# A two-layer attention kernel: an earlier first pair, later second-layer weights, a split last pair, and checks summed on ScalarE

## The chip, the cores and the metric

The kernel runs on one core of a Trainium2 chip. The metric is device time in microseconds (us), from the first to the last instruction of a run, and a median of several runs is quoted. All runs in this document, of both kernels and of every experiment, were in the fast state, so no slow run had to be set aside. The span of a profile is about 2 us shorter than the time of the same run; spans are compared with spans and times with times.

Five engines matter: TensorE (PE, and PEld for its weight loads), VectorE (DVE), ScalarE (ACT), SyncE (SP, which issues most transfers here) and the DMA engines. A wait of one engine for another is a semaphore wait. The profile also records the clock that TensorE was *granted*, as a share of full speed: 1.00 is full clock, 0.50 is half clock. A *fall* is a change from full to half.

## The reference

Two layers of the same form, one after the other, on four images of 128 channels by 96 x 96 positions. Every position attends to the 48 x 48 pooled keys of its image:

```python
g     = maxpool2(conv1x1(x, g_w, g_b))          # 64 channels, 2304 keys
theta = conv1x1(x, theta_w, theta_b)            # 64 channels, 9216 queries
phi   = maxpool2(conv1x1(x, phi_w, phi_b))      # 64 channels, 2304 keys
f     = einsum('bqc,bck->bqk', theta, phi)
y     = einsum('bqk,bkc->bqc', softmax(f), g)
W_y   = conv1x1(y, W_w, W_b)
inv   = bn_gamma * rsqrt(bn_var + BN_EPS)
out   = W_y * inv + (bn_beta - bn_mean * inv) + x
```

## The kernel before

The work is cut into 8 blocks (4 images times 2 layers, in an order that lets the layers of different images alternate). A block is 9 *pairs*; a pair is 1024 queries, held as two halves of 512 on the two halves of the partitions. A pair runs through 18 key tiles of 128 keys, two per step, so 9 steps. A step issues the score matmuls of two key tiles, their exponentials on ScalarE, the running sum of exponentials on VectorE, and one step later the value matmuls. Scores go to a PSUM pool of two buffers, so scores k + 2 need exponential k to be done.

When a pair ends, the next pair's first steps carry its ending: sum over keys (`denominators`), reciprocals and product (`normalise`), and four steps later the output projection (`project`). In the same place the keys of the next block are made bit by bit: 24 *chunks* of pooled projections, then *spread* into the layouts that the matmuls want. I call this place the *border* between two pairs.

```python
        def denominators(self):
            ps = ps_misc.tile([P, QT], F32, tag="misc", name=f"den_ps_{self.name}")
            for h in range(2):
                nc.tensor.matmul(ps[ts(h, CI), :], lhsT=ones, rhs=self.sum[:, ts(h, QT)],
                                 start=True, stop=True)
            self.rc = work.tile([P, QT], F32, tag="rc", name=f"rc_{self.name}", bufs=1)
            nc.scalar.copy(self.rc, ps)

        def normalise(self):
            rc, n = self.rc, self.number
            self.y = y = self.halves[:, :QT]
            nc.vector.tensor_add(y, y, self.halves[:, QT:])
            for i in range(QT // P):
                nc.vector.reciprocal(rc[:, ts(i, P)], rc[:, ts(i, P)])
            nc.vector.tensor_mul(y, y, rc)
            nc.vector.tensor_reduce(rmax[:, n : n + 1], rc, AX.X, ALU.max)   # checks
            nc.vector.tensor_reduce(rmin[:, n : n + 1], rc, AX.X, ALU.min)
# ... (the main loop, t counts steps of all pairs)
            if j == J_PROJECT and q:          # J_PROJECT = 4
                pairs[q - 1].project()
            if t <= total:
                for k in range(j * KB, (j + 1) * KB):
                    pairs[q].values(k)
            if j == J_WINDOW:                 # J_WINDOW = 0
                others = list(steps.pop(q % NP, [])) if q < len(pairs) else []
                if q:
                    pairs[q - 1].denominators()
                for step in others[:1]:
                    step()
                if q + 1 < len(pairs):
                    pairs[q + 1].theta()
                for step in others[1:]:
                    step()
                if q:
                    pairs[q - 1].normalise()
```

The checks find out whether a fixed shift of the exponent was safe for every query. If they fail, a general kernel runs afterwards; with these inputs it never does.

The instructions of TensorE, VectorE and ScalarE are issued in the order in which the program states them in the loop (it asks for a manual schedule). What stands early in the program therefore stands early in its engine's queue.

Of the kernel before, what the change touches and what calls it, by code (L numbers as in the profile page):

```python
# [37 lines left out]
CHUNKS = 3  # L38
ORDER = ((0, 0), (1, 0), (0, 1), (2, 0), (1, 1), (3, 0), (2, 1), (3, 1))
# [5 lines left out]
def shifted_blocks(ctx: ExitStack, tc: tile.TileContext, x: bass.AP, layers, out: bass.AP, flag):  # L45
# [26 lines left out]

    ident = const.tile([P, P], F32, name="ident")
# [7 lines left out]
    rmax = const.tile([P, len(ORDER) * NP], F32, name="rmax")  # L81
    rmin = const.tile([P, len(ORDER) * NP], F32, name="rmin")

    def load_x(b):
        xt = xp.tile([C, HW], F32, tag="x", name=f"x_{b}")
        src = x[b].rearrange("c h w -> c (h w)")
        n = 6
        for i in range(n):
            nc.sync.dma_start(out=xt[:, ts(i, HW // n)], in_=src[:, ts(i, HW // n)])
        return xt  # L90
# [4 lines left out]
    def column(src, name):  # L95
        t = const.tile([src.shape[0], 1], F32, name=name)
        nc.scalar.dma_start(out=t, in_=as_column(src))
        return t
# [10 lines left out]
    def load_layer(l, p):  # L109
        w = {}  # L110
        nat = prep.tile([CI, C], F32, tag="thnat", name=f"theta_nat_{l}")
        nc.scalar.dma_start(out=nat, in_=p["theta_w"])
        w["theta"] = transposed(nat, CI, C, f"thetaT_{l}")
        bias = const.tile([2 * CI, 1], F32, name=f"theta_b_{l}")
        for i in range(2):
            nc.scalar.dma_start(out=bias[ts(i, CI), :], in_=as_column(p["theta_b"]))
        w["theta_b"] = bias

        nat = prep.tile([2 * CI, C], F32, tag="wnat", name=f"gphi_nat_{l}")
        for i, key in enumerate(("g", "phi")):  # L120
            nc.scalar.dma_start(out=nat[ts(i, CI), :], in_=p[f"{key}_w"])
        w["gphi"] = transposed(nat, 2 * CI, C, f"gphiT_{l}")
        g_b = const.tile([P, CI], F32, name=f"g_b_{l}")
        nc.scalar.dma_start(
            out=g_b, in_=p["g_b"].rearrange("(o c) -> o c", o=1).to_broadcast((P, CI))
        )
        w["g_b"] = g_b

        W_b = column(p["W_b"], f"W_b_{l}")
        gamma = column(p["bn_gamma"], f"gamma_{l}")  # L130
        beta = column(p["bn_beta"], f"beta_{l}")
        mean = column(p["bn_mean"], f"mean_{l}")
        var = column(p["bn_var"], f"var_{l}")
        std = const.tile([C, 1], F32, name=f"std_{l}")
        nc.scalar.activation(std, var, AF.Sqrt, bias=eps)
        inv = const.tile([C, 1], F32, name=f"inv_{l}")
        nc.vector.reciprocal(inv, std)
        nc.vector.tensor_mul(inv, inv, gamma)
        shift = const.tile([C, 1], F32, name=f"shift_{l}")
        nc.vector.tensor_sub(shift, W_b, mean)  # L140
        nc.vector.scalar_tensor_tensor(shift, shift, inv, beta, op0=ALU.mult, op1=ALU.add)
        w["shift"] = shift

        W_nat = prep.tile([C, CI], F32, tag="Wnat", name=f"W_nat_{l}")
        nc.scalar.dma_start(out=W_nat, in_=p["W_w"])
        W_bn = prep.tile([C, CI], F32, tag="Wbn", name=f"W_bn_{l}")
        nc.vector.tensor_scalar(W_bn, W_nat, inv, None, ALU.mult)
        w["W"] = transposed(W_bn, C, CI, f"WT_{l}", twice=True)
        return w

    class Block:
# [5 lines left out]
        def begin_keys(self):  # L157
            name = self.name
            self.gphi = kvp.tile([P, NK], F32, tag="gphi", name=f"gphi_{name}", bufs=1)
            self.phi = kvp.tile([P, NK], F32, tag="phi", name=f"phi_{name}")  # L160
            self.gT = kvp.tile([P, NKT, CI], F32, tag="gT", name=f"gT_{name}")
            self.centre = kvp.tile([P, 1], F32, tag="centre", name=f"centre_{name}")

        def pooled(self, r):

            ps = ps_misc.tile([P, QT], F32, tag="misc", name=f"gphi_ps_{self.name}_{r}")
            for h in range(2):
                nc.tensor.matmul(  # L168
                    ps[ts(h, CI), :CC], lhsT=self.w["gphi"][:, ts(h, CI)],
# [9 lines left out]
        def spread(self, i):  # L179
# [3 lines left out]
            gphi, phi, centre = self.gphi, self.phi, self.centre  # L183
            keys = ts(i, GT * KT)
            if i == 0:
                nc.vector.tensor_reduce(centre[CI:, :], gphi[CI:, keys], AX.X, ALU.add)  # L186
                nc.vector.tensor_scalar(
                    centre[CI:, :], centre[CI:, :], -1.0 / (GT * KT), None, ALU.mult
                )
# [3 lines left out]
            nc.scalar.copy(phi[:CI, keys], phi[CI:, keys])  # L193
            ps = ps_misc.tile([P, QT], F32, tag="misc", name=f"gT_ps_{self.name}_{i}")
            for j in range(GT):
                nc.tensor.transpose(
                    ps[:, ts(j, CI)], gphi[:CI, ts(i * GT + j, KT)], ident[:CI, :CI]
                )
            nc.vector.tensor_tensor(
                self.gT[:, ts(i, GT), :],  # L200
                ps[:, : GT * CI].rearrange("p (t c) -> p t c", c=CI),
                self.w["g_b"].rearrange("p (o c) -> p o c", o=1).to_broadcast((P, GT, CI)),
# [3 lines left out]
        def key_steps(self):  # L206

            steps = {}
            for r in range(HW // CC):
                steps.setdefault(r // CHUNKS, []).append(lambda r=r: self.pooled(r))  # L210
            for i in range(NKT // GT):
                last = ((i + 1) * GT * KT * 4 // CC - 1) // CHUNKS
                steps.setdefault(last + 1, []).append(lambda i=i: self.spread(i))
            return steps

    class Pair:


        def __init__(self, blk, p, number):
            self.blk, self.p, self.number = blk, p, number  # L220
            self.name = f"{blk.name}_{p}"
            self.es = {}

        def theta(self):
            ps = ps_misc.tile([P, QT], F32, tag="misc", name=f"theta_ps_{self.name}")
            for h in range(2):
                nc.tensor.matmul(  # L227
                    ps[ts(h, CI), :], lhsT=self.blk.w["theta"],
# [3 lines left out]
            nc.scalar.activation(self.th, ps, AF.Identity, bias=self.blk.w["theta_b"])  # L232

        def scores(self, k):
# [14 lines left out]
            elif k > 1:  # L249
                nc.vector.tensor_add(self.sum, self.sum, e)  # L250

        def values(self, k):
            if k == 0:
                self.av = ps_av.tile([P, PT], F32, tag="av", name=f"av_{self.name}")
            e = self.es.pop(k)
# [7 lines left out]
            if k == NKT - 1:  # L263
# [3 lines left out]
        def denominators(self):  # L267
            ps = ps_misc.tile([P, QT], F32, tag="misc", name=f"den_ps_{self.name}")
            for h in range(2):
                nc.tensor.matmul(  # L270
                    ps[ts(h, CI), :], lhsT=ones, rhs=self.sum[:, ts(h, QT)],
                    start=True, stop=True,
                )
            self.rc = work.tile([P, QT], F32, tag="rc", name=f"rc_{self.name}", bufs=1)
            nc.scalar.copy(self.rc, ps)  # L275

        def normalise(self):
            rc, n = self.rc, self.number
            self.y = y = self.halves[:, :QT]
            nc.vector.tensor_add(y, y, self.halves[:, QT:])  # L280
            for i in range(QT // P):
                nc.vector.reciprocal(rc[:, ts(i, P)], rc[:, ts(i, P)])  # L282
            nc.vector.tensor_mul(y, y, rc)  # L283
            nc.vector.tensor_reduce(rmax[:, n : n + 1], rc, AX.X, ALU.max)  # L284
            nc.vector.tensor_reduce(rmin[:, n : n + 1], rc, AX.X, ALU.min)  # L285

        def project(self):
# [4 lines left out]
            for c in range(2):  # L292
                for h in range(2):
                    nc.tensor.matmul(  # L294
                        pss[h][ts(c, CI), :], lhsT=self.blk.w["W"][ts(h, CI), ts(c, CI)],
                        rhs=self.y[ts(h, CI), :], start=True, stop=True,
                    )
            for h in range(2):
                dst = self.blk.xt[:, ts(2 * self.p + h, QT)]
                nc.vector.scalar_tensor_tensor(  # L300
                    dst, pss[h], self.blk.w["shift"], dst, op0=ALU.add, op1=ALU.add
# [5 lines left out]
    xs = {0: load_x(0)}  # L307
    ws = [load_layer(l, p) for l, p in enumerate(layers)]
# [6 lines left out]
    def begin(n):  # L315
# [5 lines left out]
        blocks[n].begin_keys()  # L321

    begin(0)
    steps = blocks[0].key_steps()
    for n in sorted(steps):
        for step in steps[n]:
            step()

    pairs = [Pair(blk, p, n * NP + p) for n, blk in enumerate(blocks) for p in range(NP)]
    pairs[0].theta()  # L330
    total = len(pairs) * NB
    engines = {mybir.EngineType.PE, mybir.EngineType.DVE, mybir.EngineType.Activation}
    with tc.manual_schedule(engines=engines):
        for t in range(total + NB):
            if t < total:
                q, j = divmod(t, NB)
                if q % NP == 0 and j == 0 and q // NP + 1 < len(blocks):
                    begin(q // NP + 1)
                    steps = blocks[q // NP + 1].key_steps()
                for k in range(j * KB, (j + 1) * KB):  # L340
                    pairs[q].scores(k)
            if t == 0:
                continue
# [3 lines left out]
            if t <= total:  # L347
                for k in range(j * KB, (j + 1) * KB):
                    pairs[q].values(k)
            if j == J_WINDOW:  # L350
                others = list(steps.pop(q % NP, [])) if q < len(pairs) else []
# [8 lines left out]
                if q:  # L360
                    pairs[q - 1].normalise()

    bad = const.tile([P, 2], F32, name="bad")
    nc.vector.tensor_reduce(bad[:, 0:1], rmax, AX.X, ALU.max)
    nc.vector.tensor_scalar(bad[:, 0:1], bad[:, 0:1], 1.0 / SUM_MIN, None, ALU.is_gt)
    nc.vector.tensor_reduce(bad[:, 1:2], rmin, AX.X, ALU.min)
    nc.vector.tensor_scalar(bad[:, 1:2], bad[:, 1:2], 1.0 / SUM_MAX, None, ALU.is_lt)
    ps = ps_misc.tile([P, QT], F32, tag="misc", name="bad_ps")
    nc.tensor.matmul(ps[:1, :2], lhsT=ones[:, :1], rhs=bad, start=True, stop=True)
# [307 lines left out]
```

## Time and profile before

| | before |
|---|---|
| time, median of 3 runs | 2666.67 us (2666.65 to 2666.72) |
| span of the profile | 2666.4 us |
| TensorE busy | 2607.6 us, 98% |
| mean granted TensorE clock | 0.998 |
| period of a pair in the loop, most borders | 36.35 us |
| first exponential starts | 57.02 us |

The prediction shows the page's busy shares, the chain and the borders. Two rows of the table of costliest groups complete it. The columns are line, engine, operation, output<-input, shapes and count; then busy time in us and mean ns of one; then the engine's idle time just before them and what ended it.

```profile
L238 PE MATMUL sc<-theta,phi 64*64 64x512 f32 x10368 | 1234.2, 591 | 6.4 <-ACT exp L244 5.1
L258 PE MATMUL av<-exp,gT 64*64 64x512 f32 x10368 | 1228.8, 589 | 0.0
```

Scores and values are 2463 us of TensorE's 2608, both with nearly the same mean duration, 591 and 589 ns, and TensorE sat idle before the scores for 6.4 us only, in the whole kernel. These two means are worth keeping in mind: a TensorE matmul on a lower clock shows here.

### The profile page before, as it was taken

To read this page: it belongs to the slowest core of one execution; us is meant where nothing else is said; L and a number is where in the kernel's file an instruction comes from. 1 tells how busy PE (TensorE), PEld (TensorE's weight loads), DVE (VectorE), ACT (ScalarE), POOL (GpSimd) and SP (SyncE) were. 2 spreads that over 40 slices of the span, in tenths; PEclk is the share of its full clock that TensorE was granted. 3 is DMA by queue.
4 is the path that set the end of the run, shared out by engine and by line. 5 is a ranking of instruction groups with operands and counts; after the bars stand their busy time and mean duration, and the time that the engine had idled before them with its cause. 6 is when DMAs were issued, how large, how long until landed. Compare 5 with 4: busy or idle time off the path is not lost.

```text
span 2666.4 us, 51928 instructions
## 1 busy us (share of the span) xinstructions
PE 2607.6 (98%) x22808; PEld 896.0 (34%) x22808; DVE 2131.1 (80%) x2203; ACT 1576.9 (59%) x1564; POOL 0.7 (0%) x6
## 2 busy tenths in 40 slices
PE   5999999999999999999999999999999999999998
PEld 1333333333333333333333333333333333333332
DVE  3788787888877888787888778888787887888887
ACT  2655665656656656555665666655665656666664
POOL 0000000000000000000000000000000000000000
PEclk9999999999999999999999999999999999999999
DMA  6000000000000000100000000000000000000000
GB/s 218 1 1 1 1 1 1 1 1 1 1 9 17 17 17 12 77 1 1 1 1 11 15 17 17 17 1 1 1 1 1 17 17 9 17 17 17 17 17 26
DMA packets 11690, 41.48 MB, mean 16 GB/s; under 512 B 3392, under 2 KB 3776, under 8 KB 11456
## 3 DMA queue, kind: packets, MB, share of 16 engines
q1 hardware_dynamic: 8640, 37.75, 3.6%
q8 instruction: 180, 2.95, 0.5%
q10 hardware_dynamic: 2816, 0.34, 0.1%
q14 instruction: 54, 0.44, 0.1%
HBM read 19.21 MB, written 18.87 MB: 14 GB/s over the span
## 4 chain that ended last, share of the span: by engine, by line
PE 95%; ACT 3%; DMA 1%; DVE 1%; issue 0%; ACTq 0%
PE sc L238 42%; PE av L258 41%; PE gphi_ps L168 4%; PE theta_ps L227 3%; PE den_ps L270 3%; PE W_ps L294 2%; ACT theta L232 1%; DMA W_nat<-in_L_conv_W_w_dram 0%; ACT exp L244 0%; DVE centre L186 0%; ACT phi L190 0%; DVE gphi L172 0%; ACT phi L193 0%; DMA theta_b<-in_L_conv_theta_b_dram 0%; DMA theta_nat<-in_L_conv_theta_w_dram 0%
## 5 line engine op out<-in xcount | busy, mean ns | idle before, releaser
L244 ACT ACTIVATE exp<-sc,nshift 128x1024 f32<-128x1024 f32 x1296 | 1375.0, 1112 | 805.5 <-PE sc L238 805.3
L250 DVE TENSOR_TENSOR sum<-sum,exp 128x1024 f32<-128x1024 f32 x1152 | 1410.0, 1224 | 233.1 <-ACT exp L244 142.1
L238 PE MATMUL sc<-theta,phi 64*64 64x512 f32 x10368 | 1234.2, 591 | 6.4 <-ACT exp L244 5.1
L258 PE MATMUL av<-exp,gT 64*64 64x512 f32 x10368 | 1228.8, 589 | 0.0
L258 PEld LDWEIGHTS av<-exp,gT 64*64 64x64 f32 x10368 | 396.3, 133 | 716.1 <-issue 695.0
L238 PEld LDWEIGHTS sc<-theta,phi 64*64 64x64 f32 x10368 | 387.8, 133 | 726.4 <-issue 698.2
L282 DVE RECIPROCAL rc<-rc 128x128 f32<-128x128 f32 x288 | 243.4, 907 | 0.0
L172 DVE TENSOR_REDUCE gphi<-gphi_ps 128x96 f32<-128x384 f32 x192 | 107.0, 558 | 124.2 <-PE gphi_ps L168 123.5
L248 DVE TENSOR_TENSOR sum<-exp,exp 128x1024 f32<-128x1024 f32 x72 | 88.2, 1225 | 137.7 <-ACT exp L244 137.7
L168 PE MATMUL gphi_ps<-x,gphiT 128*64 128x384 f32 x768 | 160.5, 502 | 8.9 <-DVE gphi L172 0.7
L300 DVE SCALAR_TENSOR_TENSOR x<-W_ps,shift,x 128x512 f32<-128x512 f32 x144 | 101.0, 743 | 0.5 <-PE W_ps L294 0.5
L275 ACT COPY rc<-den_ps 128x512 f32<-128x512 f32 x72 | 42.2, 587 | 98.3 <-PE den_ps L270 98.3
L265 ACT COPY halves<-av 128x1024 f32<-128x1024 f32 x72 | 72.9, 1012 | 34.4 <-PE av L258 34.4
L232 ACT ACTIVATE theta<-theta_ps,theta_b 128x512 f32<-128x512 f32 x72 | 49.5, 687 | 69.4 <-PE theta_ps L227 69.2
L168 PEld LDWEIGHTS gphi_ps<-x,gphiT 128*64 128x64 f32 x768 | 48.7, 137 | 124.1 <-ACT theta L232 45.2
L227 PE MATMUL theta_ps<-x,thetaT 128*64 128x512 f32 x288 | 77.2, 614 | 3.4 <-ACT rc L275 1.2
L294 PE MATMUL W_ps<-halves,WT 64*64 64x512 f32 x576 | 75.7, 596 | 5.0 <-DVE halves L283 5.0
L270 PE MATMUL den_ps<-sum,ones 128*64 128x512 f32 x288 | 77.7, 618 | 0.0
L283 DVE TENSOR_TENSOR halves<-halves,rc 128x512 f32<-128x512 f32 x72 | 49.8, 692 | 2.5
L280 DVE TENSOR_TENSOR halves<-halves 128x512 f32<-128x512 f32 x72 | 49.1, 682 | 1.6 <-ACT halves L265 1.6
L284 DVE TENSOR_REDUCE rmax<-rc 128x1 f32<-128x512 f32 x72 | 48.9, 678 | 0.0
L285 DVE TENSOR_REDUCE rmin<-rc 128x1 f32<-128x512 f32 x72 | 48.6, 676 | 0.0
(45 smaller groups left out, 153.8 us busy)
## 6 DMA issues: line engine op xcount, KB each, us to landing
x<-in_x_dram SPq DMA_DIRECT2D x24, 768.0 KB, 9.1
out_dram<-x SPq DMA_DIRECT2D x36, 512.0 KB, 2.6
theta_nat<-in_L_conv_theta_w_dram ACTq DMA_DIRECT2D x2, 32.0 KB, 5.2
theta_b<-in_L_conv_theta_b_dram ACTq DMA_DIRECT2D x4, 0.2 KB, 5.9
gphi_nat<-in_L_conv_g_w_dram ACTq DMA_DIRECT2D x2, 32.0 KB, 5.3
gphi_nat<-in_L_conv_phi_w_dram ACTq DMA_DIRECT2D x2, 32.0 KB, 4.9
g_b<-in_L_conv_g_b_dram ACTq DMA_DIRECT2D x2, 32.0 KB, 5.1
W_nat<-in_L_conv_W_w_dram ACTq DMA_DIRECT2D x2, 32.0 KB, 6.8
```

The source lines that it names most:

```text
L168: nc.tensor.matmul(ps[ts(h, CI), :CC], lhsT=self.w["gphi"][:, ts(h, CI)], rhs=self.xt[:, ts(r, CC)], start=True, stop=True,)
L172: nc.vector.tensor_reduce(self.gphi[:, ts(r, CC // 4)].rearrange("p (h w) -> p h w", w=W // 2), ps[:, :CC].rearrange("p (h a w b) -> p h w ...
L227: nc.tensor.matmul(ps[ts(h, CI), :], lhsT=self.blk.w["theta"], rhs=self.blk.xt[:, ts(2 * self.p + h, QT)], start=True, stop=True,)
L238: nc.tensor.matmul(ps[ts(c, CI), ts(h, QT)], lhsT=self.blk.phi[ts(h, CI), ts(2 * k + c, CI)], rhs=self.th[ts(h, CI), :], start=True, stop= ...
L244: nc.scalar.activation(e, ps, AF.Exp, bias=nshift)
L248: nc.vector.tensor_add(self.sum, self.es[0], e)
L250: nc.vector.tensor_add(self.sum, self.sum, e)
L258: nc.tensor.matmul(self.av[ts(h, CI), ts(r, QT)], lhsT=self.blk.gT[ts(r, CI), k, :], rhs=e[ts(r, CI), ts(h, QT)], start=(k == 0), stop=(k ...
L270: nc.tensor.matmul(ps[ts(h, CI), :], lhsT=ones, rhs=self.sum[:, ts(h, QT)], start=True, stop=True,)
L282: nc.vector.reciprocal(rc[:, ts(i, P)], rc[:, ts(i, P)])
L294: nc.tensor.matmul(pss[h][ts(c, CI), :], lhsT=self.blk.w["W"][ts(h, CI), ts(c, CI)], rhs=self.y[ts(h, CI), :], start=True, stop=True,)
L300: nc.vector.scalar_tensor_tensor(dst, pss[h], self.blk.w["shift"], dst, op0=ALU.add, op1=ALU.add)
```

## The change

Its intent: fill the start, the end and VectorE's load. The first pair begins when 8 of the 24 chunks of keys are there, and the other 16 are made inside it. The whole program now runs under the manual schedule, SyncE included, where before only the loop did. The second layer's weights are prepared in the main loop. The last pair sums its denominators before its last values and goes out in two column halves. And the two check reductions of each pair leave VectorE: ScalarE sums denominators and reciprocals as by-products (`accum_out`) of passes over the same tile, one that was a copy before and one that is new. The diff, cut to its core:

```diff
         def denominators(self):
...
             self.rc = work.tile([P, QT], F32, tag="rc", name=f"rc_{self.name}", bufs=1)
-            nc.scalar.copy(self.rc, ps)
+            if self.last:
+                self.inverses(ps)
+            n = self.number
+            nc.scalar.activation(
+                self.th if self.last else self.rc, ps, AF.Identity,
+                accum_out=dens[:, n : n + 1],
+            )
+        def note(self):
+            n = self.number
+            to = self.th if self.last else self.rc
+            nc.scalar.activation(to, self.rc, AF.Identity, accum_out=recs[:, n : n + 1])
 
         def normalise(self):
-            rc, n = self.rc, self.number
             self.y = y = self.halves[:, :QT]
             nc.vector.tensor_add(y, y, self.halves[:, QT:])
-            for i in range(QT // P):
-                nc.vector.reciprocal(rc[:, ts(i, P)], rc[:, ts(i, P)])
-            nc.vector.tensor_mul(y, y, rc)
-            nc.vector.tensor_reduce(rmax[:, n : n + 1], rc, AX.X, ALU.max)
-            nc.vector.tensor_reduce(rmin[:, n : n + 1], rc, AX.X, ALU.min)
+            self.inverses(self.rc)
+            nc.vector.tensor_mul(y, y, self.rc)
+            self.note()
...
-    begin(0)
-    steps = blocks[0].key_steps()
-    for n in sorted(steps):
-        for step in steps[n]:
-            step()
...
+    begin(0, FIRST_GT)
+    b0 = blocks[0]
+    ws[0].make_gphi()
+    b0.pooled(0)
+    b0.pooled(1)
+    b0.pooled_2(2)
+    b0.spread_phi(0)
+    ws[0].make_theta()
+    pairs[0].theta()
+    b0.pooled_2(4)
+    b0.pooled_2(6)
+    b0.spread_phi(1)
+    b0.spread_g(0)
+    between = {0: 8, 1: 12, 3: 16, 4: 20}
+    after = {
+        0: [lambda: b0.spread_g(1)],
...
+        NB: [ws[1].make_gphi, ws[1].make_theta],
+        2 * NB: [ws[1].make_shift],
+        2 * NB + 1: [ws[1].make_W],
+    }
...
+            if t == total - 1:
+                pairs[-1].denominators()
+            if t == total:
+                break
...
+    pairs[-1].finish(check, result)
```

## The prediction

> **What bounds the kernel now.** I read the page first: busy shares, then the chain of work that ended last.
>
> ```profile
> PE 2607.6 (98%) x22808; PEld 896.0 (34%) x22808; DVE 2131.1 (80%) x2203; ACT 1576.9 (59%) x1564; POOL 0.7 (0%) x6
> ...
> PE 95%; ACT 3%; DMA 1%; DVE 1%; issue 0%; ACTq 0%
> ```
>
> TensorE (PE) is busy for 2607.6 of 2666.4 us and is 95% of the chain. All other idle time together is 58.8 us, 2.2% of the span. So whatever shortens the start and the end can save 2.2% at the very most, and anything that makes TensorE wait inside the loop is paid in full. I therefore looked at three places: the start, the end, and one border between two pairs.
>
> The start, from the chain in order of time:
>
> ```profile
> 20.01 9.17 DMA W_nat<-in_L_conv_W_w_dram
> ...
> 29.52 0.42 PE WT_ps L102
> 29.93 5.80 PE gphi_ps L168 x20
> ...
> 55.73 1.28 ACT L244
> 57.02 1.12 ACT exp L244
> ```
>
> All weights of both layers are prepared before the first chunk of keys (29.9 us), all 24 chunks are made before the first score, and the first exponential runs at 57.02. The first five chunks take 5.80 us, against 1.51 us for two (0.76 each) later: TensorE starts at half speed.
>
> A border between two pairs, from the timeline (the whole argument rests on it):
>
> ```profile
> 1193.92 1.95 PE L238 MATMUL sc<-theta,phi 64*64 64x512 f32 x16
> ...
> 1195.08 2.12 ACT L244 ACTIVATE exp<-sc,nshift 128x1024 f32<-128x1024 f32 x2 [2.00 <-PE sc L238]
> 1195.11 3.38 DVE L282 RECIPROCAL rc<-rc 128x128 f32<-128x128 f32 x4
> ...
> 1195.69 1.90 PE L258 MATMUL av<-exp,gT 64*64 64x512 f32 x16
> ...
> 1197.40 1.90 PE L238 MATMUL sc<-theta,phi 64*64 64x512 f32 x16
> ...
> 1198.52 0.69 DVE L283 TENSOR_TENSOR halves<-halves,rc 128x512 f32<-128x512 f32 x1
> ...
> 1199.12 1.04 PE L258 MATMUL av<-exp,gT 64*64 64x512 f32 x8
> ```
>
> Columns are start, duration, engine, line. Scores 4 and 5 start at 1193.92, exponentials 4 and 5 at 1195.08, and scores 6 and 7 at 1197.40 because the exponentials have freed the two score buffers in PSUM (the pool has two). The normalisation of the pair before runs on VectorE meanwhile and ends at 1198.52 + 0.69 = 1199.21. Here nobody waits for it.
>
> The same kernel has one border per block where ScalarE is held up: it must first shift the keys by a centre that VectorE computes.
>
> ```profile
> 1156.53 1.95 PE L238 MATMUL sc<-theta,phi 64*64 64x512 f32 x16
> 1158.30 1.90 PE L258 MATMUL av<-exp,gT 64*64 64x512 f32 x16
> 1160.86 2.09 PE L238 MATMUL sc<-theta,phi 64*64 64x512 f32 x16 [0.67 <-ACT exp L244]
> 1162.77 1.90 PE L258 MATMUL av<-exp,gT 64*64 64x512 f32 x16
> ```
>
> In the same view exponential 4 starts there only at 1159.69. Scores 6 follow it by 1.17 us and the value matmuls by 3.08 us (1162.77 - 1159.69). Without the delay they would start 1199.12 - 1193.92 = 5.20 us after scores 4, at 1161.73; that border lost 1.04 us. So a late ScalarE does reach TensorE, and 1.17 and 3.08 are the measured rule.
>
> **What the Trainium skill says.** "TensorE: Matmul & The Clock Gate", section "Architectural detail: the array is 16× 32×32, not 1× 128×128", says that the queues of ScalarE and VectorE are strictly first in, first out. The border just shown agrees: exponentials whose scores were there stood behind the shift that waited. The same page, section "What's actually happening", puts TensorE at half clock after an idle window of about 3.4 us that runs freely. The trace agrees: idle from about 2651.8, the granted clock falls from 1.00 to 0.50 at about 2656.2, and the last eight projection records take 1.98 us there, against 1.04 in the loop. "ScalarE: Activation LUTs", section "What ACT_TABLE_LOAD costs", gives 186 ns + 0.833 ns per element, 93 ns more for a pointer operand, and 1283 ns per table load. The trace has 587 ns for a copy of 512 columns, 687 ns with a bias, and 1.28 us per load. What the accumulator output costs, neither says.
>
> **The change part by part.**
>
> *Checks on ScalarE.* VectorE loses two reductions per pair (678 + 676 ns). It was not the bound, so this gains nothing. ScalarE gains one pass over the reciprocals per pair. The compiled order of the changed kernel shows where:
>
> ```
> L313 Activation rc, dens <- den_ps
> L265 Activation theta <- theta_ps
> L325 Activation rc, recs <- rc       [waits DVE, Activation]
> L277 Activation exp 4 <- sc 4        [waits PE]
> ```
>
> The pass stands ahead of exponentials 4 and 5 and waits for VectorE. It also writes the reciprocals in place, and the product that ends the normalisation reads them, so it must wait for that product as well, to 1199.21. (In the compiled program of the first such border it waits for VectorE's count 73, the same count on which the projection, which reads the product, waits.) In the border above: handover 0.04 us (the gap between centre and shift in the trace), pass 0.65 us (an estimate from 587 and 687 ns), so exponential 4 starts at about 1199.90 instead of 1195.08. By the rule the value matmuls start at 1199.90 + 3.08 = 1202.98 instead of 1199.12: **3.86 us lost**. The borders with other extra work give nearly the same by the same steps: with the centre 1163.74 + 3.08 - 1162.77 = 4.05; with the second part of the keys (product at 1271.72, value matmuls at 1272.33) 3.85; without keys, in the last block (reciprocals from 2625.17, scores 4 at 2623.98), 3.86. Only where the third part is spread and no chunk is made (product at 1341.51, value matmuls at 1343.37) it is 2.60. There are 71 such borders, 7 of the last kind: 64 x 3.86 + 7 x 2.60 = **265 us**. Later work can't win it back: the rest of a pair runs at the pace of TensorE.
>
> *The clock.* TensorE would idle from 1197.59 to 1199.90 + 1.17 = 1201.07, 3.48 us. That is barely one window of 3.41 us (the page's 4096 cycles), so a complete idle window falls into few gaps; each would cost about 1.7 us (half of 3.41). If a tenth did, I get some **8 us** over 71 borders (2 to 60).
>
> *Denominators.* The copy out of PSUM becomes an activation with accumulator, about 0.15 us longer (687 - 587, plus something for the accumulator). The theta matmul takes that buffer next; its weight load already waits for the copy at 56 borders. About 60 x 0.15 = **9 us**.
>
> *The start.* Layer 1's weights leave it, the first pair needs 8 chunks, and ScalarE still issues a dozen transfers and loads two tables. With weights at about 4 us, four chunks at half speed (1.3 each), ScalarE free at about 14, then two shifts, theta: first exponential at about 17.6 instead of 57.02, 39 us earlier. Given back inside the first pair: 16 chunks of 0.65 us (10.4), transposes and weights (2.5), and waits of a loop with extra work on all engines (5, a guess). Net **-22 us**. The 24 chunks of the next block are only packed differently (4 in six borders).
>
> *The end.* Before, 15.6 us pass from the last value matmuls (2650.8) to the end, of which the reciprocals take 3.38. Now they run beside the last value matmuls, but two more denominator matmuls (0.86) precede those. Projection, addition and store in halves overlap a little. I take **-2 us**; the 6 us from the flag (2660.5) to the end stay.
>
> Sum: 2666.7 + 265 + 8 + 9 - 22 - 2 = about **2925 us**, 9.7% slower.
>
> **The rivals.**
> - *The wait is hidden and only start and end count*: 2666.7 - 24 = 2643, within 2%. For it speaks ScalarE's 59% load. Against it: its idle time lies in the wrong place, and the order of a strict queue decides, not the average.
> - *The pass waits for the reciprocals alone*, not for the product: exponentials start 0.6 us earlier, 71 x 0.6 = 43 us less, 2880. The in-place write and the count speak against it.
> - *Nearly every gap trips the clock*: 71 x 1.7 to 3.4 us more, 3035 to 3160. The gap sits at the limit, so this is the large risk upwards.
> - *VectorE was the hidden bound*, and its 1.36 us per pair come back: 98 us. Against it: in the loop the view of waits shows TensorE itself waiting for ScalarE (4.0 us) and never for VectorE; the weight loads that wait for VectorE's sums before the denominators run ahead of the matmuls.
>
> **Range and chances.** The pass (0.1 us either way, 7 us in all), the accumulator (8), start and end (6) and the clock (0 to 60) give 2890 to 2975. Slower by over 2% needs only a quarter of the stall; I give it 0.92. Within 2%, if the stall is hidden, 0.05. Faster by over 2% would need nearly all of TensorE's idle time, 0.03.
>
> **What would show it.** Right: at each border exponential 4 starts just after the new pass, the pass idles on the product of the normalisation for about 5 us, TensorE idles 3.5 us waiting for the exponential (some 230 us in all where it now shows 4.0), the pair takes about 40.2 us instead of 36.4, and the first exponential is at 15 to 20 us. Wrong: exponentials 4 and 5 still start 1.2 us after their scores, or the pass waits for nothing; then the time lies near 2643. A granted clock of 0.5 after the gaps would show the third rival.

## The result, and the profile after

| | before | after |
|---|---|---|
| time, median of 4 runs each | 2666.69 us (2666.65 to 2667.74) | 3041.53 us (3037.84 to 3042.95) |
| ratio of fast runs | | 1.1402 (95%: 1.1383 to 1.1422) |
| span of the profile | 2666.4 us | 3040.8 us |
| mean granted clock | 0.998 | 0.950 |
| first exponential | 57.02 us | 24.71 us |
| first scores to second pair's first scores | 55.76 to 89.33 us | 22.66 to 81.30 us |
| second to last pair | 2526.67 us | 2904.49 us |
| last pair's first scores to the end | 50.37 us | 54.97 us |

A ratio here is the mean time of one kernel's fast runs over that of the other's of the same rounds, so it is not quite the ratio of the quoted medians.

The kernel is 14.0% slower. The prediction said slower, with 2925 us, but the time lies 66.5 us above the upper end of its range, 2975. The table says where the time is: the second pair starts 8.0 us earlier, the loop from there to the last pair takes 377.8 us longer, and the last pair with the end 4.6 us longer (it holds one more border). The sum is 374.4.

The same rows of the page as before, with the busy line and the row of the new pass (L325):

```profile
PE 2760.7 (91%) x22822; PEld 894.1 (29%) x22822; DVE 2057.1 (68%) x2067; ACT 1636.2 (54%) x1786; POOL 0.7 (0%) x6
...
L271 PE MATMUL sc<-theta,phi 64*64 64x512 f32 x10368 | 1335.1, 634 | 235.0 <-ACT exp L277 235.0
L291 PE MATMUL av<-exp,gT 64*64 64x512 f32 x10368 | 1259.8, 603 | 0.0
...
L325 ACT ACTIVATE rc<-rc 128x512 f32<-128x512 f32 x71 | 44.7, 629 | 363.4 <-DVE halves L331 363.4
```

There are two things to see. The new pass costs only 44.7 us of ScalarE, but ScalarE stood idle for 363.4 us before it, waiting for VectorE's product (L331), and TensorE waited 235.0 us for exponentials where it was 5.1. That is the predicted wait, at nearly the predicted size (some 230). But TensorE is also *busier*: 2760.7 us against 2607.6, with practically the same number of instructions. The scores' mean rose from 591 to 634 ns and the values' from 589 to 603. No instruction became larger; the granted clock fell.

A border in the middle of the kernel, from the timeline (start and duration in us, engine, line, count of records; in brackets the idle time before and its releaser):

```profile
1352.54 1.95 PE L271 MATMUL sc<-theta,phi 64*64 64x512 f32 x16
...
1357.14 0.69 DVE L331 TENSOR_TENSOR halves<-halves,rc 128x512 f32<-128x512 f32 x1
1357.93 0.63 ACT L325 ACTIVATE rc<-rc 128x512 f32<-128x512 f32 x1 [6.24 <-DVE halves L331]
1358.46 0.19 ACT L325 ACTIVATION_READ_ACCUMULATOR rc<-rc 128x1 f32 x1
1358.56 2.10 ACT L277 ACTIVATE exp<-sc,nshift 128x1024 f32<-128x1024 f32 x2
1359.70 3.45 PE L271 MATMUL sc<-theta,phi 64*64 64x512 f32 x16 [3.50 <-ACT exp L277]
```

The scores of 1352.54 are ready by about 1354.5. Their exponentials start at 1358.56, right behind the pass, which starts 0.10 us after the product has ended (1357.14 + 0.69 = 1357.83). TensorE idles 3.50 us. Then the next sixteen score records take 3.45 us where the same sixteen took 1.95 us before the gap. Busy time and granted clock of TensorE in four stretches of 3.41 us, the period with which the clock's changes fall in this trace (columns: stretch, length, busy time and count, clock, DMA share, GB/s):

```profile
1352.54:1355.96 3.42, 3.42 (x34) 1.00 0.00 0
1355.96:1359.37 3.41, 0.24 (x4) 1.00 0.00 0
1359.37:1362.78 3.41, 3.08 (x16) 0.50 0.03 5
1362.78:1366.20 3.42, 3.42 (x36) 1.00 0.00 0
```

The gap does not fill a stretch: TensorE was busy for 0.24 us of the second one. Yet the third was granted half the clock. And this is no rarity at the edge; here is another border where the gap was only 2.08 us (TensorE stopped 1.33 us into the stretch that starts at 1902.09):

```profile
1902.09:1905.50 3.41, 1.33 (x18) 1.00 0.00 0
1905.50:1908.91 3.41, 3.41 (x16) 0.50 0.02 5
```

A stretch with 1.33 us of work in it, 39%, was followed by one at half clock. Over the whole trace there are 68 times at half clock, each but the last one or two stretches long, 304.8 us together. Before had 12.5 us, all at the end. (Each of these sums, and those below, runs some 2 us past the last instruction, and the record of the clock begins only at 24.75 us here and at 34.79 before.) Each of the 68 falls followed a stretch at full clock, and the busy share of that stretch was between 0.01 and 0.42. Not one was wholly idle.

At the start, VectorE's order inside the first pair shows another loss, which matters later:

```profile
26.86 1.23 DVE L281 TENSOR_TENSOR sum<-exp,exp 128x1024 f32<-128x1024 f32 x1 [3.65 <-ACT exp L277]
28.00 1.48 DVE L192 TENSOR_REDUCE gphi<-gphi_ps 128x96 f32<-128x384 f32 x3
29.53 0.87 PE L188 MATMUL gphi_ps<-x,gphiT 128*64 128x384 f32 x4 [1.83 <-DVE gphi L192]
```

VectorE waits 3.65 us for exponentials, sums them, and only then takes the maxima of chunks that were already in PSUM. TensorE waits behind it for a free buffer.

### The profile page after: what moved, and what is told of

The parts are those of the page before. It is cut to its first block, busy times and chain, and to the rows that moved or that the text cites. A ratio compares the mean times of both kernels' runs of the same rounds, so it can differ in the third digit from the quotient of the medians.

```text
span 3040.8 us, 51534 instructions
## 1 busy us (share of the span) xinstructions
PE 2760.7 (91%) x22822; PEld 894.1 (29%) x22822; DVE 2057.1 (68%) x2067; ACT 1636.2 (54%) x1786; POOL 0.7 (0%) x6
## 4 chain that ended last, share of the span: by engine, by line
## 5 line engine op out<-in xcount | busy, mean ns | idle before, releaser
L271 PE MATMUL sc<-theta,phi 64*64 64x512 f32 x10368 | 1335.1, 634 | 235.0 <-ACT exp L277 235.0
L291 PE MATMUL av<-exp,gT 64*64 64x512 f32 x10368 | 1259.8, 603 | 0.0
L325 ACT ACTIVATE rc<-rc 128x512 f32<-128x512 f32 x71 | 44.7, 629 | 363.4 <-DVE halves L331 363.4
L313 ACT ACTIVATE rc<-den_ps 128x512 f32<-128x512 f32 x71 | 42.4, 597 | 98.1 <-PE den_ps L305 98.1
L331 DVE TENSOR_TENSOR halves<-halves,rc 128x512 f32<-128x512 f32 x71 | 49.1, 692 | 2.4
L214 ACT ACTIVATE phi<-gphi,centre 64x768 f32<-64x768 f32 (+1 forms) x27 | 23.2, 859 | 28.4 <-DVE centre L213 21.0
```

Of the source, the lines that this page charges most:

```text
L271: nc.tensor.matmul(ps[ts(c, CI), ts(h, QT)], lhsT=self.blk.phi[ts(h, CI), ts(2 * k + c, CI)], rhs=self.th[ts(h, CI), :], start=True, stop= ...
L291: nc.tensor.matmul(self.av[ts(h, CI), ts(r, QT)], lhsT=self.blk.gT[ts(r, CI), k, :], rhs=e[ts(r, CI), ts(h, QT)], start=(k == 0), stop=(k ...
```

## The experiments

Eight kernels ran in two calls. The first four share one chip and the runs of the kernel before on it (median 2667.66 us, 2663.38 to 2671.46, 15 runs); the other four share another (2666.77 us, 2661.99 to 2669.2, 16 runs). All eight gave correct results. An earlier form of e3, with a tile of its own for the pass, did not build for want of on-chip memory and became the form below (that build is not on record).

My theory: the place of the new pass in ScalarE's queue costs everything, in two ways, a direct wait and a clock that falls in the gap it leaves. Rivals: that the other parts of the change (start, second layer's weights, end) cost something; that only a gap that fills a whole stretch of 3.41 us trips the clock; that the clock is a side show and the direct wait larger than I worked out; that relieving VectorE is worth something by itself.

### e1: the pass four steps later

```diff
@@ normalise
             nc.vector.tensor_mul(y, y, self.rc)
-            self.note()
@@ main loop
             if j == J_PROJECT and q:
+                pairs[q - 1].note()
                 pairs[q - 1].project()
```

> The changed kernel with ScalarE's pass over the reciprocals issued four steps later, when VectorE has long finished. My theory (the pass stands ahead of two exponentials in ScalarE's queue and waits for the normalisation; the gap that this makes in TensorE also drops its clock) expects the whole loss of the loop to go: 2655 to 2672 us, TensorE waiting under 10 us for exponentials in the loop, and half clock in the trace for under 30 us instead of 305. Rival, that the extra ScalarE work or the accumulator itself costs the time: still over 2900. Rival, that start and end lost it: the same, over 2900.

Measured: 2665.39 us (2663.11 to 2669.19, 12 runs), ratio to before 0.9994 (0.9985 to 1.0003). The clock is back at 0.997. A border of this kernel, from the timeline:

```profile
1332.04 2.11 ACT L277 ACTIVATE exp<-sc,nshift 128x1024 f32<-128x1024 f32 x2
...
1333.91 0.69 DVE L331 TENSOR_TENSOR halves<-halves,rc 128x512 f32<-128x512 f32 x1
1334.15 1.90 PE L271 MATMUL sc<-theta,phi 64*64 64x512 f32 x16
...
1344.13 0.63 ACT L325 ACTIVATE rc<-rc 128x512 f32<-128x512 f32 x1
```

The exponentials no longer wait for the product: they start 1.87 us before it. The pass runs ten microseconds after it, when its input has long been there, and nobody waits. One line moved in the program takes 376 us back (3041.53 - 2665.39). So the whole loss was the place of the pass, and the work of the checks on ScalarE is nearly free. In the loop the period of most pairs is 36.45 us, against 36.35 before; e5 shows that this 0.10 us is what the accumulator in `denominators` leaves on the path.

It also shows what the rest of the change is worth: 2.3 us by the medians, which the interval doesn't tell from nothing. In its trace the second pair starts 13.6 us earlier than before (75.71 against 89.33), the loop takes 8.9 us longer (2535.56 against 2526.67), and the last pair with the end 0.6 us less (49.75 against 50.37).

### e2: the checks alone, on the kernel before

```diff
@@ denominators
-            nc.scalar.copy(self.rc, ps)
+            n = self.number
+            nc.scalar.activation(self.rc, ps, AF.Identity, accum_out=dens[:, n : n + 1])
@@ normalise
-            nc.vector.tensor_reduce(rmax[:, n : n + 1], rc, AX.X, ALU.max)
-            nc.vector.tensor_reduce(rmin[:, n : n + 1], rc, AX.X, ALU.min)
+            nc.scalar.activation(rc, rc, AF.Identity, accum_out=recs[:, n : n + 1])
```

(and the judging of the sums at the end, as in the change.)

> The kernel before with the checks on ScalarE and nothing else. If the checks carry the whole loss and the other parts gave some 8 us back at the start: 3040 to 3058 us, with the same gaps of 3.4 to 3.5 us. If the new first pair or the new order of the other engines is needed for the loss: near 2667.

Measured: 3054.39 us (3050.06 to 3056.08), ratio 1.1455 (1.1436 to 1.1474). The granted clock is 0.95 here too, with some 315 us at half clock. Its view of waits (total us, times, longest):

```profile
ACT rc L285 <- DVE halves L284: 362.8, 71, 6.5
```

The same 71 waits with the same total as in the changed kernel (363.4). This part alone makes the loss. The other parts together don't add to it.

### e3: the pass waits for the reciprocals only

```diff
@@ note
-            to = self.th if self.last else self.rc
+            to = self.th if self.last else self.halves[:, QT:]
             nc.scalar.activation(to, self.rc, AF.Identity, accum_out=recs[:, n : n + 1])
```

The pass now writes where the product doesn't read, into the half of `halves` that has been added already, so it needn't wait for the product. It still stands at the same place in the queue.

> The changed kernel, but the pass writes into a tile that nobody reads, so it waits for the reciprocals and not for the product behind them (0.69 us). My theory: the gaps shrink by about 0.6 us to 2.9, 43 us less direct waiting, and the clock still falls at most borders because a window need only be 60% idle: 2970 to 3005 us. If the clock fell only in gaps longer than its window of 3.41 us, the clock's part would go as well: 2850 to 2870. If the product were not what it waits for: 3041.

Measured: 2953.2 us (2947.79 to 2958.06), ratio 1.1075 (1.1054 to 1.1096). That is 88 us less than the changed kernel, more than I expected.

```profile
PE sc L271 <- ACT exp L277: 183.7, 71, 3.9
```

TensorE's direct wait fell from 235.0 to 183.7 us over the same 71 borders, 0.72 us each, the product's duration and handover. Most gaps are 2.78 us long now. If only gaps beyond 3.41 us tripped the clock, only the few with a longer gap would, and the time would lie at 2850 to 2870; but half-clock time is still 219 us, in 55 times. My miss was the other way: the time lies 17 us below my range of 2970 to 3005. Gaps of 2.7 to 2.8 us tripped almost as often as the longer ones, 43 of 46. But in the last block, where gaps are 1.57 us, none did, and only 7 times in the loop did half clock last two stretches, against 19 in the changed kernel.

### e4: the gaps filled with idle-time matmuls

```diff
+    def busy(q, n):
+        ps = ps_misc.tile([P, QT], F32, tag="misc", name=f"busy_ps_{q}")
+        for _ in range(n):
+            nc.tensor.matmul(ps[:CI, :], lhsT=ones, rhs=pairs[q].th, start=True, stop=True)
@@ main loop, after the values of the step
+            if j == 1 and 0 < q < len(pairs):
+                busy(q, 1 if q % NP == NP - 1 or q >= total // NB - NP else 3)
```

The order, the pass and its wait are those of the changed kernel. Nothing reads the three (or one) added matmuls per border; they only keep TensorE busy where it would idle. This takes the clock away and leaves the wait.

> The changed kernel with three idle-time matmuls (one where the gap is 2.1 us) put into each gap of TensorE; they write a buffer that nobody reads and fit into the gap. The wait itself stays. If the half clock costs about 150 us of the loss: 2885 to 2920 us with half clock for under 60 us in all. If the clock is a by-product that costs nothing (the matmuls behind the gap would wait anyway): 3035 to 3060.

Measured: 2925.35 us (2923.78 to 2928.93), ratio 1.0967 (1.0948 to 1.0985), clock 0.995, 31 us at half clock. That is 5 us above the upper end of what I expected: the clock was worth less than the 150 us I had put on it.

```profile
1308.74 2.79 PE L451 MATMUL busy_ps<-theta,ones 128*64 128x512 f32 x6
1311.16 2.10 ACT L277 ACTIVATE exp<-sc,nshift 128x1024 f32<-128x1024 f32 x2
1312.31 2.09 PE L271 MATMUL sc<-theta,phi 64*64 64x512 f32 x16 [0.78 <-ACT exp L277]
```

The gap is filled for 2.79 us, 0.78 us remain, and the scores behind it take 2.09 us instead of 3.45. Useless work made the kernel 116 us faster (3041.53 - 2925.35). That is the price of the clock, a little low, as 7 of the 68 falls are still there. What remains, 260 us (2925.35 - 2665.39), is the price of the direct wait and of those falls. By the periods of the pairs, e4 less e1:

| border | predicted loss, us | measured, us |
|---|---|---|
| most (36.45 -> 40.33) | 3.86 | 3.88 |
| with the centre (38.00 -> 42.02) | 4.05 | 4.02 |
| second part of the keys (36.97 -> 40.78) | 3.85 | 3.81 |
| third part, no chunk (34.80 -> 37.26) | 2.60 | 2.46 |
| last block (33.79 -> 36.46) | 3.86 | 2.67 |

The second row is that of the four blocks whose clock stayed up; in the three others it fell there, and the loss was 5.6 to 5.7 us. The last row was off: I had taken the border of the very last pair, which has no theta matmul, for all of the last block's.

### e5: the checks back on VectorE

From the changed kernel, the checks of all pairs but the last are again a maximum and a minimum on VectorE; start and end stay as changed.

```diff
@@ denominators
+            else:
+                nc.scalar.copy(self.rc, ps)
@@ note
-            to = self.th if self.last else self.rc
-            nc.scalar.activation(to, self.rc, AF.Identity, accum_out=recs[:, n : n + 1])
+            if self.last:
+                nc.scalar.activation(self.th, self.rc, AF.Identity, accum_out=recs)
+                return
+            nc.vector.tensor_reduce(rmax[:, n : n + 1], self.rc, AX.X, ALU.max)
+            nc.vector.tensor_reduce(rmin[:, n : n + 1], self.rc, AX.X, ALU.min)
```

(The judging of these maxima and minima also moves, to three steps before the end.)

> The changed kernel with the checks of the first 71 pairs back on VectorE as before; start and end stay as changed. If VectorE's two reductions cost nothing and the accumulator's read costs 0.1 us at 56 borders: about 6 us below the kernel with the late pass, 2655 to 2663 us, 0.2 to 0.4% under the kernel before. If VectorE's relief is worth something: slower than the kernel with the late pass.

Measured: 2661.19 us (2655.27 to 2662.31, 13 runs), ratio 0.9976 (0.9967 to 0.9984). VectorE is at 80% here and at 77% in e1, and e5 is not slower but some 4 us faster. The two ran on different chips, so the medians alone would not carry the 4 us. The loops of the two profiles do: most pairs take 36.35 us here, as before, and 36.45 in e1, and from the second to the last pair e5 takes 2529.32 us, 6.2 less than e1. The place of the 0.10 us, first in e1 and then here:

```profile
1144.61 0.60 ACT L313 ACTIVATE rc<-den_ps 128x512 f32<-128x512 f32 x1 [1.39 <-PE den_ps L305]
1145.10 0.19 ACT L313 ACTIVATION_READ_ACCUMULATOR rc<-den_ps 128x1 f32 x1
...
1145.35 1.08 PE L260 MATMUL theta_ps<-x,thetaT 128*64 128x512 f32 x4
```

```profile
1147.14 0.59 ACT L316 COPY rc<-den_ps 128x512 f32<-128x512 f32 x1 [1.39 <-PE den_ps L307]
...
1147.77 1.08 PE L262 MATMUL theta_ps<-x,thetaT 128*64 128x512 f32 x4
```

The theta matmul starts 0.74 us after ScalarE began on the denominators in e1, behind the read of the accumulator, and 0.63 us after it here. Taking work off VectorE gained nothing: it was not the bound.

### e6: in the first pair, maxima before sums

```diff
@@ main loop
-                pairs[q].scores(k)
+                pairs[q].scores(k, late=t in between)
         if t in between:
...
+            for k in range(t * KB, (t + 1) * KB):
+                pairs[0].add(k)
```

(`late` leaves the running sum to `add`, which comes behind the chunks of that step; the diff is against e5.)

> As the one above, and in the first pair the sums of exponentials come after the maxima of the chunks in VectorE's order. My reading of the start: at four places a chunk's matmul waits 2.3 us because the maxima stand behind sums that wait for exponentials, and one of these gaps drops the clock. Then these four gaps go and the time falls by 9 to 13 us against the one above. If the start is bound by the transfers or by ScalarE instead: no change.

Measured: 2648.79 us (2647.35 to 2649.33), ratio 0.9932 (0.9915 to 0.9949), 12.4 us less than e5.

```profile
21.75 1.85 DVE L194 TENSOR_REDUCE gphi<-gphi_ps 128x96 f32<-128x384 f32 x3 [2.05 <-PE gphi_ps L190]
23.66 0.87 PE L190 MATMUL gphi_ps<-x,gphiT 128*64 128x384 f32 x4 [0.66 <-DVE gphi L194]
```

VectorE takes the maxima as the chunks come, and TensorE's wait there is 0.66 us instead of 1.83. The second pair starts at 67.28 us, against 81.09 in e5. Of these 13.8 us the first pair itself gives 10.3 (48.31 us instead of 58.63). The other 3.5 are an earlier start of its first scores (18.96 against 22.46), before anything that the edit moves; so not all of the 12.4 us is shown to come from it.

### e7: a warm TensorE at the start

```diff
+    some = work.tile([P, PT], F32, tag="halves", name="some", bufs=1)
+    nc.vector.memset(some[:, :QT], 1.0)
+    some_ps = ps_sc.tile([P, PT], F32, tag="sc", name="some_ps")
+    nc.tensor.matmul(some_ps[:CI, :QT], lhsT=ones, rhs=some[:, :QT], start=True, stop=True)
     ws[0].make_gphi()
+    nc.tensor.matmul(some_ps[:CI, :QT], lhsT=ones, rhs=some[:, :QT], start=True, stop=True)
     b0.pooled(0)
     b0.pooled(1)
-    b0.pooled_2(2)
-    b0.spread_phi(0)
     ws[0].make_theta()
+    b0.pooled_2(2)
     pairs[0].theta()
+    b0.spread_phi(0)
```

> As the one above, with two matmuls on ones while the first loads run and theta's weights made before the third chunk. If the half clock at the start costs one window's half: 2 to 5 us less. If the first loads bound it: no change.

Measured: 2644.56 us (2644.44 to 2644.88), ratio 0.9917 (0.9901 to 0.9934), 4.2 us less than e6. The two halves of the edit (warm matmuls, earlier theta weights) were not told apart.

### e8: the last pair's end

```diff
@@ denominators, last pair
-                nc.scalar.activation(self.th, ps, AF.Identity, accum_out=dens)
+                self.den_ps = ps
@@ finish
+            busy_ps = ps_sc.tile([P, PT], F32, tag="sc", name="busy_ps")
+            for _ in range(3):
+                nc.tensor.matmul(busy_ps[:CI, :QT], lhsT=ones, rhs=self.sum[:, :QT], start=True, stop=True)
             nc.scalar.copy(half, self.av[:, QT:])
+            nc.scalar.activation(self.th, self.den_ps, AF.Identity, accum_out=dens)
             nc.vector.tensor_add(y, self.av[:, :QT], half)
```

In the changed kernel the end has the same fault in small. Its timeline, from the last values on:

```profile
3025.78 1.95 PE L291 MATMUL av<-exp,gT 64*64 64x512 f32 x16
3029.38 0.60 ACT L313 ACTIVATE theta<-den_ps 128x512 f32<-128x512 f32 x1 [5.79 <-DVE rc L320]
...
3029.97 0.58 ACT L359 COPY halves<-av 128x512 f32<-128x512 f32 x1
```

The pass over the denominators waits for the reciprocals, and the copy of the finished values, ready since about 3027.7, stands behind it.

> As the one above, and in the end ScalarE copies its half of the values before it sums the denominators (it waited 2 us there behind a sum that waited for the reciprocals), and three idle-time matmuls keep TensorE's clock. Copy 1.3 us and projection 1.0 us earlier: 2 to 2.5 us less. If the end is bound by the stores alone: no change.

Measured: 2642.74 us (2642.11 to 2643.07), ratio 0.9910 (0.9894 to 0.9927), 1.8 us less than e7, a little under what I expected. The new order and the three matmuls were not told apart. In its profile TensorE is busy for 99% of the span and the mean granted clock is 1.000. It beats both kernels: 0.9% below before, 13.1% below the change.

## Why the prediction was right or wrong

**The bound and the mechanism: right.** TensorE was the bound, the pass stood ahead of the exponentials in ScalarE's queue, it waited for the product because it writes in place, and TensorE paid. e1 shows the place, e2 that the checks alone make the loss, and e3 the in-place write: without it the wait per border falls by 0.72 us. The signs named beforehand came, but for two: the pass idled 5.1 us per border (363.4 / 71), the gap was 3.50 us and the wait 235 us; a pair took 41.6 to 43.1 us at most borders instead of 40.2 (40.33 in e4, without the falls), and the first exponential came at 24.71 us instead of 15 to 20.

**The direct wait, 265 us: right.** e4 less e1 is 260; some 5 of these are falls of the clock left in e4, so the wait alone is nearer 255 (an estimate from the periods). The rule of 1.17 and 3.08 us, read from the one border per block that already was held up, gave most borders to within 0.02 to 0.04 us; the third-part and the last-block borders were 0.14 and 1.2 us too large.

**The clock, 8 us: wrong, and this alone took the result out of the range.** The step that failed is the one that says the gap of 3.48 us "is barely one window of 3.41 us (the page's 4096 cycles), so a complete idle window falls into few gaps". The gap was well predicted (3.50). But no complete idle window was needed. In all ten traces the clock fell after every recorded window at full clock in which TensorE was busy for less than 0.40. Between 0.41 and 0.52 some windows were followed by a fall and some were not (no fall after 0.41 in the changed kernel, falls after 0.45 in e4 and 0.52 at the start of e1), so there is no sharp limit in these shares. The price is 116 us (the changed kernel less e4). I took the "idle window" of the Trainium skill ("TensorE: Matmul & The Clock Gate", section "What's actually happening") for a window without any work, and I took the one fall in the trace of before, after several microseconds of idleness, for agreement. That fall couldn't tell the two readings apart.

Chance does not give the count. Take 0.42 as the limit: a window of 3.41 us trips if at least 58% of it, 1.98 us, is idle. A gap of 3.50 us stays below that only if the window's edge cuts it so that both parts are under 1.98 us, that is, if the first part is between 1.52 and 1.98 us: 0.46 of 3.41, 13% of the cases, if the edge falls anywhere with equal chance. So 87% of such gaps would trip, 65% of e3's 2.78 us, and none of 1.57 us (estimates). None of 1.57 us did, but 45 of the 46 gaps of 3.3 to 3.5 us tripped in the changed kernel, and 43 of 46 in e3. The edges do not fall by chance: from its second to its seventh block the changed kernel takes 378.9 us for nine pairs, each time to within 0.2 us, and e3 368.6, which is 111.0 and 108.0 windows of 3.413 us. So the same gaps meet the window at the same places in block after block, and a count of borders is not a count of independent trials. What makes them lock was not tested. Each fall costs about 1.9 us (116 us for the 61 falls that e4 has fewer), as some of them last two stretches.

The rival "nearly every gap trips the clock", 3035 to 3160, holds the result. I had named the gap as "at the limit" and the clock as the large risk, but I gave it no room in the range beyond 60 us.

**Denominators, 9 us: about right.** The accumulator leaves 0.10 us per pair on the path, 6.2 us in the loop (e1 less e5). e1's loop is 8.9 us longer than before in all; the rest, 2.7 us, is in e5's loop as well and lies in its first block (293.8 us for eight pairs against 291.2), where the chunks are packed otherwise and the second layer's weights are made. Which of the two it is, was not tested.

**The start, -22 us: too much.** The profile of the changed kernel shows -8.0, that of e1 with the same first pair -13.6; the five profiles with this first pair (changed, e1, e3, e4, e5) have the first exponential at 20.84 to 24.71 us and the second pair at 75.71 to 81.30, so the size is uncertain by some 5 us. Two terms were off. The first exponential came at 24.71 instead of 17.6; the record of full clock begins at 24.75 there. And the first pair gave back more: from its first scores to the second pair's it took 58.6 us against 33.6, so 25 us more, where 18 were predicted (10.4 + 2.5 + 5). e6 shows what a part of that was: VectorE's sums ahead of the chunk maxima, 10.3 us in the first pair. The "waits of a loop with extra work on all engines (5, a guess)" was the term that was too small.

**The end, -2 us: nearly nothing.** e1 shows -0.6. The copy that stands behind the pass ate the gain, and e8 got 1.8 us of it back.

**The rivals.** "Hidden" fell with the result itself. "Reciprocals alone" fell by e3, which makes just that wait and differs from the changed kernel. "VectorE was the hidden bound" fell by e5.

What stays open: the exact rule by which the clock falls. The shares were read from windows laid over the traces, with matmul ends that the profile models, and not from an experiment that sets the gap and its phase.

## What to carry to other kernels

Before moving work to an engine with spare time, look at which instruction it will stand in front of and what it waits for: a pass of 0.63 us that nobody needed soon cost 5 us per pair, because it waited in front of work that TensorE needed at once, and four steps later it cost nothing. When a bound TensorE is made to idle, count the clock as well as the gap: here gaps of about 2 to 3.5 us cost some 1.9 us more each time they tripped it, and three useless matmuls per gap took nearly all of that away. And when a page states a limit, ask what the trace in hand can tell about it; a fall after a long idle time is no evidence for where the limit lies.

## What the Trainium skill lacked or had wrong

- "TensorE: Matmul & The Clock Gate", sections "What's actually happening" and "Why this matters for your kernels": half clock after at least one idle window of about 3.4 us, and no idle gaps beyond about 3 us between matmul bursts. The period of 3.41 us agrees with these traces. But a window need not be idle: in the changed kernel the clock fell after windows with busy shares of 0.01 to 0.42 (68 falls, none at 0). The shortest gap in the loop that tripped it was 2.07 us there and 1.88 us in e4, while some gaps of 2.30 us and one of 3.50 us did not. Another section of the page, "A second HAM failure mode: psum-queue depth-cycling", does tell of short idles that made the clock swing, but gives no length or share.
- The same page, same sections, on the way back: full clock after a busy window. In the changed kernel the window need not be quite full: the clock came back after windows with a busy share of 0.84 or more, and stayed at half after shares of 0.78 or less. At the start of e3 it stayed at half after one of 0.95, so this is no sharp limit either.
- "ScalarE: Activation LUTs" names an accumulator output and not what it costs. Here it is a second instruction of 186 to 203 ns behind the pass (629 ns for 512 columns), and it put 0.10 us per pair on the path.
- No page says, as far as I looked, that matmuls whose result nobody reads are worth their time in such gaps. Here three per border (2.79 us) made the kernel 116 us faster.
